# Attention steps of three, three and two key tiles in a two-layer graph network, with half-width exponentials

## The chip, the cores and the metric

The kernel runs on one core of one Trainium2 chip. The metric is the device time of one execution in microseconds (us). TensorE (PE in the profile) does the matrix products, VectorE (DVE) and ScalarE (ACT) the elementwise work, GpSimd (POOL) some elementwise work and the requests for stores, SyncE (SP) the requests for loads.

## The reference, cut to what matters

```
h = relu(layernorm(x))                                # x: 16 graphs, 1024 nodes, 256 channels
A = 1 - 2*|sigmoid(c_j - c_i) - 0.5|                  # c: mean over channels of h
q = relu(para * (h^T @ (adj * A)))                    # 4 heads of 64 channels
k, v = h @ kv_w
x = x + softmax(q k^T * scale) v                      # attention, per graph and head
h = relu(layernorm(x))
agg = A_hat @ h;  y = relu(batchnorm(agg @ W1^T));  x = x + batchnorm(y @ W2^T)
```

All of it is in float32. The attention is 16 graphs x 4 heads x 1024 queries x 1024 keys.

## The kernel before, in words

The program has a start (layer norm, keys, values and queries of the first graph), an attention stage over all 16 graphs, and an ending in `second` (the second batch norm and the last product). This study is about the attention stage.

**Units.** A unit is one graph `b`, one pair of heads `k` and one half `f` of the queries (512 of them): 16 x 2 x 2 = 64 units. In a unit, scores are made with keys on the partitions: for each of 8 tiles of 128 keys, `scores` (matmul at L1081) multiplies the tile's keys with 512 queries, for both heads `e` and both halves `c` of the tile. The four matmuls use four 64x64 quarters of the PE array. The result `sc` is 128 partitions x 1024 numbers (head 0, head 1), two banks of PSUM. One ScalarE instruction (L1089) takes the exponential of all 1024 into an SBUF tile `p`. `Unit.values` (L1124) multiplies `p` with the values `v` and accumulates over the 8 tiles into `o`. `Unit.add` (L1110, L1113) sums the `p` tiles on VectorE for the softmax's denominator; `fold` (L1159, L1160) reduces that sum, and `sums` is a small PE product (L1173) of what is left, followed by three small VectorE operations (L1181 to L1187).

**Steps.** `attention` goes through the units in steps. A step is two key tiles, so that a unit has 4 steps and the stage has 256. The order that a step gives to PE is written out by hand: first the scores of the step's two tiles; then what stands in `at_mid` (the small `sums` product); then the values of the step before; then background products, taken from the generator `background(b)` until its cost `done` reaches what is `due` at this step; then what stands in `at_end` (the folds). ScalarE and VectorE get their instructions in the same order, and each engine works its own list strictly in order.

**Background.** While the attention of graph `b` runs, `background(b)` makes the keys (`pk`), queries (`pg`) and values (`pv`) of graph `b + 1`, and the aggregation (`pa`) and hidden layer (`py`) of graph `b - 1`. All of these go through the helper `product` (L174), which uses two 128x64 halves of the array. `weigh` makes the eight weight tiles `w` of a graph: two Abs (L508) and one Tanh (L516) on ScalarE and one product with `adj` (L495) on VectorE for each.

**Buffers.** [...] `ps_sc` holds two score tiles of two banks each, `ps_o` one, `ps_mm` three for all other products. The pool `p4` holds four buffers for `p`. A score tile's buffer is written again once the exponential that reads it has ended; a `p` buffer once the values product and the VectorE sum have read it.

```
for m in (2 * g, 2 * g + 1):                       # a step's two tiles
    sc = ps_sc.tile([P, 2, FB], ...)               # two banks
    ... four matmuls into sc ...
    pr = p4.tile([P, 2, FB], ...)
    nc.scalar.activation(pr, sc, AF.Exp)           # 1024 numbers a partition
```

A trailing part `layers(True)` is a second form of both layers that is run only if a check on the softmax sums fails; in the profiled execution it is not run.

## Time and profile before

| what | value |
|---|---|
| median of 3 runs | 2460.21 us (2460.09 to 2460.84) |
| the profiled execution, its own time | 2460.34 us |
| its span, first to last instruction | 2458.6 us |
| PE busy | 2412.4 us, 98% of the span |
| VectorE busy | 2003.9 us, 82% |
| ScalarE busy | 1257.7 us, 51% |
| GpSimd busy | 559.5 us, 23% |
| exponentials (L1089) | 512 of 1020 ns |
| score matmuls (L1081), value matmuls (L1124) | 498.6 us and 494.7 us busy |
| mean granted TensorE clock | 0.993 |

A float32 matmul of the program appears in the trace as two records, each with its own weight load, so 2048 score matmuls show as 4096. Records that run side by side in different parts of the array overlap, and "busy" is the time in which at least one runs. PE's records have a modelled end: where the end of one overlaps the start of the next, the pace is read from the starts.

The span has four stretches: the start up to 54.1 us, the first graph's attention up to about 160 us, fifteen more graphs, and from about 2150 us the ending. Graphs 2 to 13 repeat every 134.4 us almost to the nanosecond.

### The profile page before, as it was taken

What the parts mean: (1) busy time and instruction counts of PE and PEld (TensorE: products, weight loads), DVE (VectorE), ACT (ScalarE), POOL (GpSimd) and SP (SyncE); (2) the same over time, 40 slices, a digit from 0 to 9 for tenths busy, and PEclk for the clock granted to TensorE, in tenths of its full rate; (3) what the DMA queues carried; (4) which work ended last, traced back from release to release, by engine and by line L of the source; (5) the groups of instructions that cost most, each with busy time, mean ns of one, the idle gap of its engine ahead of it and who ended that gap; (6) DMA issues with size and microseconds to landing.
All of it is one profiled execution on the core that took longest, in us unless ns stands there. A gap on an engine that the chain in (4) does not pass through costs nothing. (4 is left out here: it accounts for less than half of the span.)

```text
span 2458.6 us, 35932 instructions
## 1 busy us (share of the span) xinstructions
PE 2412.4 (98%) x13290; PEld 832.6 (34%) x13290; DVE 2003.9 (82%) x3103; ACT 1257.7 (51%) x1870; POOL 559.5 (23%) x645
## 2 busy tenths in 40 slices
PE   9999999999999999999999999999999999999994
PEld 4333333333333333333333333333333332334444
DVE  5678888988888888888898888888888878767775
ACT  7874554545464545445454546454454534335554
POOL 1381202111111212020211212121202103136652
PEclk9999999999999999999999999999999999999997
DMA  4675545363645554453536355544545353456559
GB/s 146 204 242 182 172 138 179 118 229 125 209 139 193 171 189 163 158 171 126 209 117 231 120 201 160 197 164 167 172 134 188 116 201 142 152 197 230 196 193 372
DMA packets 204553, 437.18 MB, mean 178 GB/s; under 512 B 21456, under 2 KB 96720, under 8 KB 200272
## 3 DMA queue, kind: packets, MB, share of 16 engines
q1 hardware_dynamic: 173328, 327.29, 39.7%
q0 software_dynamic: 31040, 107.50, 11.6%
q8 instruction: 107, 1.75, 0.3%
q14 instruction: 78, 0.64, 0.1%
HBM read 331.36 MB, written 103.35 MB: 177 GB/s over the span
## 5 line engine op out<-in xcount | busy, mean ns | idle before, releaser
L1089 ACT ACTIVATE p<-sc 128x1024 f32<-128x1024 f32 x512 | 495.4, 1020 | 649.5 <-PE sc L1081 649.5
L1113 DVE TENSOR_TENSOR acc<-acc,p 128x1024 f32<-128x1024 f32 x384 | 469.8, 1223 | 58.2 <-ACT p L1089 36.9
L1081 PE MATMUL sc<-q,k 64*64 64x512 f32 x4096 | 498.6, 602 | 0.5 <-ACT p L1089 0.5
L1124 PE MATMUL o<-p,v 128*64 128x512 f32 x2048 | 494.7, 604 | 0.0
L174 PE MATMUL pa<-aht,h_b 128*64 128x512 f32 x1536 | 346.0, 592 | 1.1 <-ACT h_b L368 1.1
L174 PE MATMUL pg<-w,x_h 128*64 128x512 f32 x1472 | 332.0, 592 | 0.0
L1081 PEld LDWEIGHTS sc<-q,k 64*64 64x64 f32 x4096 | 131.5, 132 | 336.4 <-issue 287.8
L1124 PEld LDWEIGHTS o<-p,v 128*64 128x64 f32 x2048 | 124.6, 136 | 297.7 <-issue 251.2
L1142 POOL DMA_DIRECT2D out_d<-os x58 | 32.9, 568 | 803.2 <-DVE os L1138 803.2
L495 DVE SCALAR_TENSOR_TENSOR w<-w,adj 128x1024 f32<-128x1024 f32 x128 | 164.9, 1288 | 46.1 <-ACT w L516 45.1
L174 PEld LDWEIGHTS pa<-aht,h_b 128*64 128x64 f32 x1536 | 110.1, 137 | 220.6 <-issue 207.8
L174 PEld LDWEIGHTS pg<-w,x_h 128*64 128x64 f32 x1472 | 105.7, 137 | 210.1 <-issue 198.4
L508 ACT ACTIVATE w<-cbc,csum 128x512 f32<-128x512 f32 x256 | 170.3, 716 | 0.0
L516 ACT ACTIVATE w<-w 128x1024 f32<-128x1024 f32 x128 | 135.6, 1059 | 2.5
L571 DVE TENSOR_TENSOR w<-w,w 128x1024 f32<-128x1024 f32 x112 | 134.6, 1232 | 1.5
L174 PE MATMUL pv<-kvw_f,ht 128*64 128x256 f32 x1024 | 116.1, 379 | 0.0
L174 PE MATMUL pk<-ht,kvw_f 128*64 128x512 f32 x512 | 115.2, 593 | 0.2 <-ACT ht L430 0.2
L174 PE MATMUL py<-at,w 128*64 128x512 f32 x464 | 112.6, 593 | 0.8 <-DVE at L729 0.7
L174 PE MATMUL py<-at,w1s 128*64 128x512 f32 x448 | 107.9, 595 | 0.0
L1453 ACT ACTIVATE yin_f<-yin_f,sm_f 128x512 f32<-128x512 f32 x128 | 93.5, 803 | 19.0 <-DMA yin_f<-y_d 17.0
L826 POOL DMA_DIRECT2D y_d<-y x112 | 61.6, 550 | 145.1 <-DVE y L846 75.8
L1160 DVE TENSOR_REDUCE part<-acc 128x16 f32<-128x512 f32 x128 | 87.8, 686 | 4.4
(197 smaller groups left out, 2968.6 us busy)
## 6 DMA issues: line engine op xcount, KB each, us to landing
aht<-aht_d SPq DMA_DIRECT2D x224, 512.0 KB
adj<-in_adj_dram SPq DMA_DIRECT2D x128, 512.0 KB
y_d<-y POOLq DMA_DIRECT2D x128, 256.0 KB, 3.0
yin_f<-y_d SPq DMA_DIRECT2D x32, 1024.0 KB
para<-in_para_dram SPq DMA_DIRECT2D x64, 256.0 KB
x_d<-x_x POOLq DMA_DIRECT2D x16, 1024.0 KB, 5.1
xo_f<-x_d SPq DMA_DIRECT2D x32, 512.0 KB
out_dram<-xo_f POOLq DMA_DIRECT2D x32, 512.0 KB, 11.1
```

Of the source, the lines that this page charges most:

```text
L174: nc.tensor.matmul(dst[r], left[:, r], right, start=start, stop=stop)
L495: nc.vector.scalar_tensor_tensor(w, w, 1.0, a, op0=ALU.add, op1=ALU.mult)
L508: nc.scalar.activation(w[:, t, :].rearrange("p (t q) -> p t q", q=P), cbc[:, q * NT // NH : (q + 1) * NT // NH], AF.Abs, bias=csum[:, th * ...
L516: nc.scalar.activation(made[i], made[i], AF.Tanh, scale=-0.5 / C)
L571: nc.vector.tensor_sub(block(i)[part], block(x)[part], block(y)[part])
L826: nc.gpsimd.dma_start(out=y1_d[i][:, j, :], in_=y)
L1081: nc.tensor.matmul(sc[part, e, :], ks[b][k][r, m * P + c * HW : m * P + (c + 1) * HW], qs[b][k][r, f * FB : (f + 1) * FB], start=True, sto ...
L1089: nc.scalar.activation(pr, sc, AF.Exp)
L1113: nc.vector.tensor_add(self.acc, self.acc, pr)
L1124: nc.tensor.matmul(self.o[r, :], vs[b][k][:, m, r], pr[:, e, :], start=(m == 0), stop=(m == NT - 1),)
L1160: nc.vector.tensor_reduce(self.part[:, e, :], acc.rearrange("p (c s) -> p c s", s=SQ), AX.X, ALU.add)
L1453: nc.scalar.activation(y, y, AF.Relu, bias=sh[:, j : j + 1], scale=scale[:, j : j + 1])
```

## The change

A unit has three steps, of three, three and two key tiles, in place of four steps of two: the stage has 192 steps. `scores` now takes a PSUM buffer of one bank for each head of a tile, from a pool of four such buffers (the same four banks as before), and makes the exponential of each head by its own instruction of 512 numbers. The `p` tiles come from a pool of five buffers. The `sums` product moves from the middle of a step (after the scores) to the end of the step before it, behind the background products. In `background`, the generator `w` of the weight tiles is advanced by two slots ahead of the keys' products, and by two more with the queries' first product. `due` counts key tiles in place of steps. To make room, the transposed copies `sq` are made and stored in halves, the small tiles of `degrees` live in a part of `stats1` that is not yet in use, and the channel sums are padded in the tile that they are transposed in, by GpSimd. The second form of the layers (`shifted_attention`) takes the same buffers.

```diff
         p4 = attn.enter_context(tc.tile_pool(name=f"p4_{kind}", bufs=4, side="right"))
+        p6 = attn.enter_context(tc.tile_pool(name=f"p6_{kind}", bufs=5, side="right"))
         ps_sc = attn.enter_context(
-            tc.tile_pool(name=f"ps_sc_{kind}", bufs=2, space=PSUM, side="right")
+            tc.tile_pool(name=f"ps_sc_{kind}", bufs=4, space=PSUM, side="right")
         )
...
-            for k in range(CC):
-                sq = p1.tile([P, N], F32, tag="sq", name=f"sq_{b}_{k}")
+            for q in range(2 * CC):
+                k, i = divmod(q, 2)
+                sq = p1.tile([P, FB], F32, tag="sq", name=f"sq_{b}_{q}")
...
-                nc.gpsimd.dma_start(out=hsq_d[b][:, k], in_=sq)
-                for _ in range(3):
+                nc.gpsimd.dma_start(out=hsq_d[b][:, k, i * FB : (i + 1) * FB], in_=sq)
+                for _ in range(2):
                     yield 0.0
...
-            nc.vector.transpose(turned, wides[b])
+            nc.gpsimd.memset(turned[:, NT:], 0.0)
+            nc.gpsimd.tensor_copy(turned[:, :NT], csums[b])
+            nc.vector.transpose(turned, turned)
...
+        GROUPS = (0, 1, 2), (3, 4, 5), (6, 7)
...
             yield from weave(islice(products, 6), (0, islice(w, 2)))
-            yield from weave(islice(products, 3), (0, islice(w, 1)))
+            yield from weave(islice(products, 3), (0, islice(w, 2)))
             gathered(b, 1)
-            yield from weave(islice(products, 3), (0, islice(w, AHEAD - 3)))
+            yield from weave(islice(products, 2), (0, islice(w, AHEAD - 4)))
...
                 w, products, norm = weighers[b + 1], keys_values(b + 1), normed(b - 1)
+                yield from islice(w, 2)
                 yield from weave(islice(products, 4), (0, islice(w, 4)))
                 asked = queries(b + 1)
-                yield from weave(islice(asked, 7), (0, double(w)))
+                yield from weave(islice(asked, 7), (1, double(w)))
...
-            for m in (2 * g, 2 * g + 1):
-                sc = ps_sc.tile([P, 2, FB], F32, tag="sc", name=f"sc_{b}_{k}_{f}_{m}")
+            for m in GROUPS[g]:
+                pr = p6.tile([P, 2, FB], F32, tag="p", name=f"p_{b}_{k}_{f}_{m}")
                 for e in range(2):
+                    sc = ps_sc.tile([P, FB], F32, tag="sc", name=f"sc_{b}_{k}_{f}_{m}_{e}")
                     r = slice(e * HD, (e + 1) * HD)
                     for c in range(2):
                         part = slice(c * HW, (c + 1) * HW)
                         nc.tensor.matmul(
-                            sc[part, e, :],
+                            sc[part, :],
...
-                pr = p4.tile([P, 2, FB], F32, tag="p", name=f"p_{b}_{k}_{f}_{m}")
-                nc.scalar.activation(pr, sc, AF.Exp)
+                    nc.scalar.activation(pr[:, e, :], sc, AF.Exp)
                 made.append(pr)
...
-                    due = total * (s % per_graph + 1) / per_graph
+                    whole = CC * NH * NT
+                    past = (NH * unit.at[1] + unit.at[2]) * NT + GROUPS[g][-1] + 1
+                    due = total * past / whole
...
-                            wait = 6 if opens else 4
-                            at_mid.setdefault(s + 3 + opens, []).append(last.sums)
+                            wait = 5 if opens else 3
+                            at_end.setdefault(s + 2 + opens, []).append(last.sums)
```

More of the change, by code (lines that the diff above doesn't have):

```diff
@@ L124, in layers @@
         invs = {}
-        csums, wides, cbcs, weighted, weighers, steps = {}, {}, {}, {}, {}, {}
+        csums, cbcs, weighted, weighers, steps = {}, {}, {}, {}, {}
         s1s = {}
@@ L202, in layers @@
         nc.sync.dma_start(out=kvw, in_=kv_w.rearrange("(k p) j -> p k j", p=P))
-        rows = big.tile([P, NH, NT], F32, name="rows")
+        spare = stats1[:, HC - 1].rearrange("p a s -> p (a s)")[:, (B * NH - 10) * 6 :]
+        rows = spare[:, : NH * NT].rearrange("p (q t) -> p q t", t=NT)
         def columns_of(col, name):
@@ L227, in load_adj_t @@
             return tile_
-        deg_sm = big.tile([P, 6, NT], F32, name="deg")
+        dinv = big.tile([P, NT], F32, name="dinv")
         later = {}
-        row, diag, col, deg, tmp_deg, dinv = (deg_sm[:, i, :] for i in range(6))
+        row, diag, col, deg, tmp_deg = (
+            spare[:, (NH + i) * NT : (NH + i + 1) * NT] for i in range(5)
+        )
         def degrees():
@@ L331, in __init__ @@
                 if first:
-                    wide = p2.tile([P, SQ], F32, tag="csum", name=f"csum_{b}")
-                    nc.gpsimd.memset(wide[:, NT:], 0.0)
-                    wides[b] = wide
-                    self.csum = csums[b] = wide[:, :NT]
+                    self.csum = csums[b] = p2.tile([P, NT], F32, tag="csum", name=f"csum_{b}")
                 if early:
@@ L432, in squares @@
         def squares(b):
-            for k in range(CC):
-                sq = p1.tile([P, N], F32, tag="sq", name=f"sq_{b}_{k}")
+            for q in range(2 * CC):
+                k, i = divmod(q, 2)
+                sq = p1.tile([P, FB], F32, tag="sq", name=f"sq_{b}_{q}")
+                cols = slice(q * HW, (q + 1) * HW)
                 nc.vector.transpose(
-                    sq.rearrange("p (i t s) -> p i t s", i=NS, s=SQ),
-                    hs["a", b][:, :, k * P : (k + 1) * P].rearrange("p t (i s) -> p i t s", s=SQ),
-                )
-                nc.gpsimd.dma_start(out=hsq_d[b][:, k], in_=sq)
-                for _ in range(3):
+                    sq.rearrange("p (i t s) -> p i t s", t=NT, s=SQ),
+                    hs["a", b][:, :, cols].rearrange("p t (i s) -> p i t s", s=SQ),
+                )
+                nc.gpsimd.dma_start(out=hsq_d[b][:, k, i * FB : (i + 1) * FB], in_=sq)
+                for _ in range(2):
                     yield 0.0
@@ L1031, in shifted_attention @@
                     name = f"{b}_{hd}_{t}"
-                    sc = ps_sc.tile([P, N], F32, tag="sc", name=f"sc_{name}")
+                    scs = [
+                        ps_sc.tile([P, FB], F32, tag="sc", name=f"sc_{name}_{g}") for g in range(NH)
+                    ]
                     for g in range(NH):
                         nc.tensor.matmul(
-                            sc[:, g * FB : (g + 1) * FB],
+                            scs[g],
                             qs[b][k][r, t * P : (t + 1) * P],
@@ L1040, in shifted_attention @@
                         )
-                    sm = p2.tile([P, 3], F32, tag="smx", name=f"smx_{name}")
-                    nc.vector.tensor_reduce(sm[:, 0:1], sc, AX.X, ALU.max, negate=True)
-                    pr = p4.tile([P, N], F32, tag="p", name=f"p_{name}")
-                    nc.scalar.activation(
-                        pr, sc, AF.Exp, bias=sm[:, 0:1], accum_out=sm[:, 1:2]
-                    )
-                    nc.vector.reciprocal(sm[:, 2:3], sm[:, 1:2])
-                    pt = p4.tile([P, N], F32, tag="p", name=f"pt_{name}")
+                    sm = p2.tile([P, 6], F32, tag="smx", name=f"smx_{name}")
+                    for g in range(NH):
+                        nc.vector.tensor_reduce(sm[:, g : g + 1], scs[g], AX.X, ALU.max, negate=True)
+                    nc.vector.tensor_tensor(sm[:, 2:3], sm[:, 0:1], sm[:, 1:2], op=ALU.min)
+                    pr = p6.tile([P, N], F32, tag="p", name=f"p_{name}")
+                    for g in range(NH):
+                        nc.scalar.activation(
+                            pr[:, g * FB : (g + 1) * FB],
+                            scs[g],
+                            AF.Exp,
+                            bias=sm[:, 2:3],
+                            accum_out=sm[:, 3 + g : 4 + g],
+                        )
+                    nc.vector.tensor_add(sm[:, 5:6], sm[:, 3:4], sm[:, 4:5])
+                    nc.vector.reciprocal(sm[:, 2:3], sm[:, 5:6])
+                    pt = p6.tile([P, N], F32, tag="p", name=f"pt_{name}")
                     for g in range(NH):
@@ L1119, in values @@
                     self.o = ps_o.tile([P, FB], F32, tag="o", name=f"o_{self.name}")
-                for i, pr in enumerate(prs):
-                    m = 2 * g + i
+                for m, pr in zip(GROUPS[g], prs):
                     for e in range(2):
@@ L1130, in values @@
                         )
-                if g == NG - 1:
+                if g == len(GROUPS) - 1:
                     self.os = p2.tile([P, FB], F32, tag="os", name=f"os_{self.name}")
@@ L1242, in attention @@
             units = [Unit(b, k, f) for b in range(B) for k in range(CC) for f in range(NH)]
+            NG = len(GROUPS)
             steps = [(u, g) for u in units for g in range(NG)]
@@ L1260, in attention @@
                     made = scores(*unit.at, g)
-                    due = total * (s % per_graph + 1) / per_graph
+                    whole = CC * NH * NT
+                    past = (NH * unit.at[1] + unit.at[2]) * NT + GROUPS[g][-1] + 1
+                    due = total * past / whole
                     if b == B - 1:
-                        due -= 0.5 * min(s % per_graph + 1, (per_graph - 1 - s % per_graph) * 0.75)
+                        due -= 0.25 * min(past, (whole - past) * 0.75)
                 else:
```

## The prediction

> **What bounds the kernel now.** I read the page's engine line first, then the busy time of three stretches of one graph each.

> ```profile
> PE 2412.4 (98%) x13290; PEld 832.6 (34%) x13290; DVE 2003.9 (82%) x3103; ACT 1257.7 (51%) x1870; POOL 559.5 (23%) x645
> ```
> ```profile
> 698.40:832.80 134.40, 134.40 (x782) 43.38 (x780) 115.67 (x179) 68.21 (x104) 22.62 (x31) 1.00 0.49 168
> 832.80:967.10 134.30, 134.30 (x778) 43.37 (x776) 115.65 (x179) 68.10 (x104) 22.52 (x31) 1.00 0.50 169
> ```

> In the second fence the columns are the stretch, its length, then busy us of PE, PEld, DVE, ACT, POOL. PE is busy for all of 134.4 us: in the steady graphs nothing but PE's own work sets the time. ScalarE (68 us) and VectorE (116 us) have room. The waits of PE show how little it waits for ScalarE in the whole run:

> ```profile
> PE sc L1081 <- ACT p L1089: 0.5, 1, 0.5
> ```

> But busy PE is not PE at its pace. The timeline of one step, us from the span's start, length, engine:

> ```profile
> 1001.12 1.95 PE L1081 MATMUL sc<-q,k 64*64 64x512 f32 x16
> ...
> 1002.28 1.94 ACT L1089 ACTIVATE p<-sc 128x1024 f32<-128x1024 f32 x2 [3.44 <-PE sc L1081]
> 1003.00 1.94 PE L1124 MATMUL o<-p,v 128*64 128x512 f32 x8
> ...
> 1004.77 5.32 PE L174 MATMUL pg<-w,x_h 128*64 128x512 f32 x24
> ...
> 1010.02 1.95 PE L1081 MATMUL sc<-q,k 64*64 64x512 f32 x16
> ```

> The weight loads of `pg` in that timeline start at 1004.34, 1004.77, 1005.20: one pass of 512 columns each 0.429 us. The starts then price a step. Scores, 4 passes: 1003.00 - 1001.12 = 1.88, so 0.16 over 4 x 0.429. Values, 4 passes: 1.77, 0.05 over. Background, 12 passes: 5.25, 0.10 over. **A step costs 0.31 us beyond its passes**, at the changes between the 64x64 and the 128x64 shape of the array.

> The last thing to see is the one wait of PE for an exponential. In the first unit two steps follow each other with no work between, so a third score tile stands behind two full buffers:

> ```profile
> 54.09 1.95 PE L1081 MATMUL sc<-q,k 64*64 64x512 f32 x16
> ...
> 55.47 1.92 ACT L1089 ACTIVATE p<-sc 128x1024 f32<-128x1024 f32 x2
> 56.52 0.21 PEld L1081 LDWEIGHTS sc<-q,k 64*64 64x64 f32 x8 [1.37 <-ACT p L1089]
> 56.52 2.00 PE L1081 MATMUL sc<-q,k 64*64 64x512 f32 x16 [0.49 <-ACT p L1089]
> ```

> The third tile was due at 54.09 + 4 x 0.429 + 0.05 = 55.85 and began at 56.52, 0.05 us after the first exponential's own record ended (56.47). That is what every three-tile step of the changed kernel will meet, in halves.

> [...] the four quarters start 7 ns apart, but no run here shows two halves of a tile started half a microsecond apart. [...]

> **Part 1: fewer steps (a gain).** 64 units x 1 step less x 0.31 us = 20 us off PE, all on the path. The passes are the same. Bounds 18 to 20.5.

> **Part 2: the third tile (a loss).** Six one-bank scores are asked for in one go, four banks exist, PE works in order. Time from a step's first score:
> - Tile 0's exponential starts at 1.16 (1002.28 - 1001.12) for both heads, so about 1.15 for head 0 alone.
> - A 512-wide exponential is not in the trace. From copies out of PSUM, 128x256 takes 376 ns and 128x512 584, so 512 elements are 0.416 us and the exponential 1.02 - 0.42 = 0.60. Two neighbours take 1.92, not 2.04, so the next starts 0.12 before the end, 0.48 after the start. [...]
> - Head 0 is read from 1.15 to 1.75, head 1 from 1.63 to 2.23. With 0.05 to answer, PE may write the two banks at 1.80 and 2.28.
> - They are due at 1.77. Head 0 is on time; **head 1 is 0.50 late**. Its weight load, no longer hidden, adds the 0.05 seen in the 2.00 us of the waiting pair above against 1.95. I take 0.54; bounds 0.45 (part of the load hidden)[...].

> Two of a unit's three steps have three tiles: 128 steps x 0.54 = 69 us. Behind the waiting score on PE stand the values of the step before and all background; nothing may pass. A two-tile step fits its four banks and waits for nothing.

> **Part 3: ScalarE late at a step's start.** What stands ahead of a three-tile step's exponentials now adds to PE's time one for one. The trace of before has such places: in graphs 2 to 13 the first exponential starts 1.83 us after its score in a graph's second step and 3.72 in the third, all others within 1.64. Asking for the weights ahead of the keys takes that away. In the changed order the second step has ahead of it three weight tiles (2.3 us each by the starts of L508 and L516) and four copies (0.48), 8.9 us, done by 13.7 after the step before began (the last copy waits for its product at 12.2); PE needs 3.3 for scores, 1.8 for values and 8.6 for background = 13.7 and the exponential can start 1.15 later. So 0 there, and if it fails at most 2.5 x 16 = 40. In the first graph the third step stands behind 5.5 weight tiles, four `k` copies and two of `ht`, about 3.3 us late: with its neighbours 5 us once, bounds 0 to 12.

> **Part 4: `sums` at a step's end.** It costs the same two changes of work less one of shape: scores and values with it between take 3.76 us now (at 1035.03) against 3.65. I take 0, bounds -2 to +2. But it is asked for about one and a half steps after the last fold instead of two. VectorE starts its sums at most 5.8 us behind the exponentials' ends (over all tiles of the trace), the fold takes 1.4 (two of 0.69), and the two-tile step between takes some 8; only in the first and the last two graphs, with steps of 5 to 7 us, can PE wait for it: 2 us, bounds 0 to 10.

> **Part 5: work beside PE.** ScalarE: 1024 x 0.48 against 512 x 0.90, 31 us more of 1200 idle. In the second of the three-tile steps the third `p` waits for the values of the step before (five buffers, six tiles): ScalarE stands about 1 us with copies of background products behind it, which have three `ps_mm` banks of 1.7 us each as cover. Transposes in halves: 52 x 0.70 for 26 x 1.24, 4 us of VectorE; 26 stores more on GpSimd's queue, 15 us of 1900 idle. GpSimd's padding puts up to 1 us ahead of one VectorE transpose in each graph, where VectorE idles 19 us. The weight tiles' `adj` loads are asked for earlier on SP, ahead of the `para` and x loads, and needed ten us later: 0, cover the keys' products. The tiles of `degrees`: 0.

> **Sum**, against the profiled execution: 2460.3 - 20 + 69 + 5 + 2 = **2516 us**. It stands 0.1 above the median shown, so the same holds for the median. The bounds together (wait 58 to 78, saved 20.5 to 18, the rest -2 to +24) reach from 2495 to 2544.

> **Rivals.**
> - *The banks come free in time* (faster). If exponentials release a bank before 1.77 us, part 1 alone is left: 2460 - 20 = 2441. It decides at 0.16 us of wait a step (20 / 128): below that the kernel is faster. For it: head 0 is already on time. Against: no exponential of the 256 steps started before 1.15, and 0.48 + 0.60 cannot follow in 0.62. 0.08.
> - *The late half does not run beside the early one.* If head 1's passes must wait until head 0's have left the array, 0.43 more a step, 55 us: 2571. For it: such a start is not in the trace. Against: quarters run side by side and records of both heads overlap. 0.08.
> - *Late copies and sums.* Stalls of part 3 and 4 at their upper end in many graphs, some 24 us: 2540. VectorE at 86% in the steady graphs speaks for it, its idle 19 us against. 0.12.
> - *No change to tell*: 0.02 (a difference under 0.2% is about what a measurement of this kernel cannot tell from none).

> **How the numbers follow.** My forecast has 0.70. The range takes its bounds and most of the late case, 2495 to 2546, and leaves out both outer rivals. Slower by over 0.2%: 0.70 + 0.08 + 0.12 = 0.90; within 0.02; faster 0.08.

> **What would show it.** In the changed profile: the wait of `sc` for the exponential `p` on PE, from one to some 128 in number, adding to 60 to 75 us of later starts (the view shows less, since a record's modelled end covers 0.2); values starting about 3.27 us after a three-tile step's first score; exponentials of 0.60 us; a steady graph of 134.4 - 1.25 + 4.3 = 137.5 us; 192 steps with 0.31 between passes. A steady graph under 134 would refute part 2, one near 141 would mean the second rival, waits for VectorE on PE the third.

## The result: slower, and by far more than predicted

The changed kernel takes **2654.15 us** (median of 4 runs, 2651.01 to 2655.58) against 2460.21 us for the kernel before: a ratio of 1.0786, 95% interval 1.0767 to 1.0805. The profiled execution took 2651.01 us, its span is 2649.1 us. The prediction was 2516 us with a range of 2495 to 2546. The sign was right; 138 us of loss were not foreseen.

The engine line of the page after, and the busy time of graphs 5 and 6 (the stretch, its length, busy us of PE, PEld, DVE, ACT, POOL, then the granted clock, the DMA share and GB/s):

```profile
PE 2496.1 (94%) x13290; PEld 875.1 (33%) x13290; DVE 2030.5 (77%) x3129; ACT 1296.2 (49%) x2382; POOL 569.6 (22%) x685
```
```profile
782.13:927.72 145.59, 140.02 (x779) 46.12 (x778) 117.83 (x182) 70.74 (x136) 24.54 (x34) 0.98 0.45 156
927.72:1072.62 144.90, 139.19 (x779) 45.89 (x776) 118.13 (x182) 70.97 (x136) 24.61 (x34) 0.99 0.47 157
```

Three things differ from the two lines shown of before. A steady graph takes 145 us in place of 134.4; the forecast was 137.5. PE is no longer busy all the time: 5.6 us of each graph are gaps. And the clock is below 1.00. VectorE has only 2.2 to 2.5 us more work in a graph and idles for 27 us of it, so a rise in its work alone does not explain 10 us. From the starts of the first scores of each graph, the loss of the profiled execution, 191 us, lies here: 39.7 us in graph 0, 12.5 in graph 1, 128 in graphs 2 to 13 (10.7 each), 5.1 in graph 14, the rest behind it.

The waits of PE, in the list of waits (waiter, releaser: us in total, times, longest):

```profile
PE py L175 <- DVE y L875: 71.2, 13, 5.9
PE sums L1189 <- DVE part L1176: 20.3, 1, 20.3
PE sc L1099 <- ACT p L1106: 11.8, 7, 5.4
```

The first two were not there before. Each waits for VectorE, and the list of VectorE's own waits says what VectorE stood for:

```profile
DVE sq L441 <- DMA hsq_d<-sq: 79.8, 13, 6.5
DVE csumt L472 <- POOL csumt L471: 27.3, 1, 27.3
```

**The steady graph.** The timeline of all engines in graph 6 (start, length, engine, line, operation; in brackets the idle time before and its releaser):

```profile
1043.89 0.70 DVE L441 STREAM_TRANSPOSE sq<-x_h 128x512 f32<-128x512 f32 x1
...
1044.48 1.46 SPq L193 DMA_DIRECT2D adj<-in_adj_dram  x3
1044.88 0.56 POOL L445 DMA_DIRECT2D hsq_d<-sq  x1 [1.47 <-DVE sq L441]
...
1050.63 0.71 DVE L441 STREAM_TRANSPOSE sq<-x_h 128x512 f32<-128x512 f32 x1 [6.04 <-DMA hsq_d<-sq]
...
1051.58 1.03 PE L175 MATMUL py<-at,w1s 128*64 128x512 f32 x4
...
1052.57 4.66 DVE L1130 TENSOR_TENSOR acc<-acc,p 128x1024 f32<-128x1024 f32 x3
1057.15 0.68 DVE L875 TENSOR_TENSOR y<-py,y 128x512 f32<-128x512 f32 x1
...
1057.98 1.97 PE L175 MATMUL py<-at,w1s 128*64 128x512 f32 x4 [5.37 <-DVE y L875]
```

Read it downwards. The third half of `sq` is transposed at 1043.89 and its store asked for at 1044.88. The fourth half stands right behind it in VectorE's list and needs the same, only buffer; it starts at 1050.63, when the store has landed. Behind it VectorE still owes a fold (1.4 us) and three sums of `p` (4.66 us) before it can empty the `py` bank that PE wants: PE stands 5.37 us. The store took 5.6 us to land. The first of three loads of `adj` (512 KB each) went out 0.4 us ahead of it, the others within 0.6 us behind it; in all 13 such graphs the third store, with these loads beside it, lands in 5.3 to 6.2 us, and the first, second and fourth land in 2.3 to 4.1. No run takes the loads away, so that they are what slows the store is likely, not shown. Three stretches of the same place have the clock, the DMA share and the GB/s in the last three columns, and show what comes after PE's gap:

```profile
1048.00:1051.00 3.00, 3.00 (x16) 1.01 (x14) 0.37 (x1) 1.51 (x4) 0.00 (x0) 1.00 0.99 382
...
1054.00:1057.00 3.00, 0.00 (x0) 0.00 (x0) 2.79 (x3) 0.00 (x0) 0.00 (x0) 1.00 0.00 0
...
1057.00:1060.00 3.00, 2.02 (x6) 0.85 (x8) 2.23 (x5) 0.00 (x0) 1.27 (x1) 0.61 0.03 5
```

The DMA engines are at 0.99 while the store is under way. After the gap the granted clock is down: the four records of `py` at 1057.98 take 1.97 us where the same four took 1.03 us at 1051.58. The granted clock is 0.50 for 3.4 or 6.8 us, by turns, once in each of graphs 1 to 13.

**Graph 0.** The timeline there:

```profile
160.65 0.58 POOL L299 DMA_DIRECT2D aht_d<-one  x1
161.22 0.14 POOL L470 MEMSET csumt<- 128x24 f32 x1
161.29 0.20 POOL L471 COPY csumt<-csum 128x8 f32<-128x8 f32 x1
...
161.52 0.21 DVE L472 STREAM_TRANSPOSE csumt<-csumt 128x32 f32<-128x32 f32 x1 [27.25 <-POOL csumt L471]
...
165.00 0.43 PE L1189 MATMUL sums<-part,same 128*64 128x32 f32 x4 [20.32 <-DVE part L1176]
```

Through the whole of VectorE's wait GpSimd is building `aht`, without a pause over 0.61 us, up to 161.22 (and goes on with it behind the padding); the padding of `csum` stands behind that in its list, VectorE's transpose stands behind the padding (in these 27.25 us VectorE runs nothing else), the fold behind the transpose, `sums` behind the fold, and all of PE behind `sums`.

**The step itself** is as forecast. A three-tile step in the timeline of PE and of its weight loads:

```profile
1009.21 3.34 PE L1099 MATMUL sc<-q,k 64*64 64x512 f32 x24
1012.48 2.79 PE L1140 MATMUL o<-p,v 128*64 128x512 f32 x12
```
```profile
1010.98 0.20 PEld L1099 LDWEIGHTS sc<-q,k 64*64 64x64 f32 x4 [0.71 <-ACT p L1106]
1011.47 0.20 PEld L1099 LDWEIGHTS sc<-q,k 64*64 64x64 f32 x4 [0.29 <-ACT p L1106]
```

Scores to values are 3.27 us, the number forecast, and the third tile's two heads load their weights at 1010.98 and 1011.47, each 0.05 us after an exponential's end (1010.93 and 1011.42).

### The profile page after: what moved, and what is told of

Read it like the earlier page. It is cut to its first block, busy times and chain, and to the rows that moved or that the text cites. A ratio compares the mean times of both kernels' runs of the same rounds, so it can differ in the third digit from the quotient of the medians.

```text
span 2649.1 us, 36668 instructions
## 1 busy us (share of the span) xinstructions
PE 2496.1 (94%) x13290; PEld 875.1 (33%) x13290; DVE 2030.5 (77%) x3129; ACT 1296.2 (49%) x2382; POOL 569.6 (22%) x685
## 3 DMA queue, kind: packets, MB, share of 16 engines
q8 instruction: 107, 1.75, 0.3%
## 5 line engine op out<-in xcount | busy, mean ns | idle before, releaser
L1106 ACT ACTIVATE p<-sc 128x512 f32<-128x512 f32 x1024 | 528.7, 605 | 582.2 <-PE sc L1099 502.8
L1099 PE MATMUL sc<-q,k 64*64 64x512 f32 x4096 | 557.4, 608 | 11.8 <-ACT p L1106 11.8
L1130 DVE TENSOR_TENSOR acc<-acc,p 128x1024 f32<-128x1024 f32 x384 | 482.1, 1256 | 76.3 <-ACT p L1106 51.4
L1140 PE MATMUL o<-p,v 128*64 128x512 f32 x2048 | 484.3, 604 | 0.0
L1099 PEld LDWEIGHTS sc<-q,k 64*64 64x64 f32 x4096 | 149.2, 132 | 345.5 <-issue 178.1
L175 PE MATMUL py<-at,w1s 128*64 128x512 f32 x448 | 121.4, 652 | 71.5 <-DVE y L875 71.2
L1127 DVE TENSOR_TENSOR acc<-p,p 128x1024 f32<-128x1024 f32 x64 | 78.6, 1229 | 82.4 <-ACT p L1106 82.3
L846 ACT ACTIVATE y<-py,vec 128x512 f32<-128x512 f32 x28 | 19.3, 688 | 226.2 <-PE py L175 226.2
L175 PE MATMUL py<-at,w 128*64 128x512 f32 x464 | 128.7, 666 | 0.8 <-DVE at L735 0.7
L369 ACT ACTIVATE h_b<-x_x,lnsm_b 128x256 f32<-128x256 f32 x128 | 70.0, 602 | 87.7 <-DVE lnsm_b L358 87.7
```

The source lines that it names most:

```text
L175: nc.tensor.matmul(dst[r], left[:, r], right, start=start, stop=stop)
L369: nc.scalar.activation(self.h[:, t, :], self.src[:, t, :], AF.Relu, bias=self.sm[:, 1, t : t + 1], scale=self.sm[:, 0, t : t + 1], accum_o ...
L1099: nc.tensor.matmul(sc[part, :], ks[b][k][r, m * P + c * HW : m * P + (c + 1) * HW], qs[b][k][r, f * FB : (f + 1) * FB], start=True, stop=True,
L1106: nc.scalar.activation(pr[:, e, :], sc, AF.Exp)
L1127: nc.vector.tensor_add(self.acc, self.held, pr)
L1130: nc.vector.tensor_add(self.acc, self.acc, pr)
```

## The experiments

The theory after this reading: three separate losses. (a) The fourth half of `sq` behind the third through one buffer: in steady graphs, with the halved clock that follows. (b) The padding on GpSimd: graph 0. (c) The third tile's bank wait, as predicted. Its rival for (a): VectorE is late because three-tile steps bunch its sums of `p`. For (b): the loads of `degrees` or the changed order of weights hold graph 0.

| kernel | median us | ratio to before, 95% | graph 0 | graph 3 |
|---|---|---|---|---|
| changed | 2654.15 | 1.0767 to 1.0805 | 145.2 | 145.8 |
| sq_in_y | 2557.27 | 1.0378 to 1.0413 | 145.5 | 137.7 |
| pad_dve | 2628.63 | 1.0665 to 1.0700 | 126.8 | 145.6 |
| both | 2532.55 | 1.0276 to 1.0310 | 121.5 | 137.7 |
| two_tile | 2462.58 | 1.0001 to 1.0018 | 105.5 | 134.4 |
| before_halves2 | 2572.33 | 1.0427 to 1.0471 | 105.5 | 143.3 |
| before_pad2 | 2491.73 | 1.0110 to 1.0144 | 136.4 | 134.4 |
| twos_first2 | 2517.54 | 1.0220 to 1.0254 | 105.9 | 137.7 |
| values_between2 | 2509.95 | 1.0186 to 1.0220 | 121.4 | 136.5 |
| late_half | 2532.17 | 1.0271 to 1.0306 | 122.2 | 137.7 |
| keys_first | 2545.12 | 1.0331 to 1.0366 | 118.7 | 138.7 |
| whole_exp | 2529.89 | 1.0265 to 1.0299 | 118.6 | 137.6 |

The last two columns are us from the first score of that graph to the first of the next. The kernel before has 105.5 and 134.4 there; graphs 2 to 13 of "both" have 137.7 but for two of 138.0 and 139.1.

**1. sq_in_y: another buffer for the halves**

```diff
-                sq = p1.tile([P, FB], F32, tag="sq", ...)
+                sq = py.tile([P, FB], F32, tag="y", ...)     # ring of seven
```

> The changed kernel with one edit: the four halves of squares take their buffer from the ring of seven y buffers of the same size instead of the single sq buffer. Theory (VectorE stands behind the store that must leave the single buffer, PE then waits for py banks and its clock is halved): the wait of the squares' transpose for its store, 80 us in 13 waits, is gone; the wait of py for L875 on PE falls from 71 us to under 8; no halved clock in graphs 2 to 13; a steady graph takes 137.4 us instead of 145.0; the sum is 12 x 7.6 and 9.5 for graph 1, so about 2654 - 100 = 2554 us. Rival (VectorE is simply late because three-tile steps bunch its sums of p): py still waits for VectorE, a steady graph stays above 142, 2610 to 2654 us.

Measured 2557.27 us, a steady graph of 137.7 us; the wait of `py` for L875 is gone, and no halved clock stands in graphs 1 to 13. The theory holds for (a): 97 us. The fourth transpose now starts 0.63 us behind the third: so close do the two writes follow each other where nothing holds the second.

**2. pad_dve: the padding off GpSimd**

```diff
-            nc.gpsimd.memset(turned[:, NT:], 0.0)
-            nc.gpsimd.tensor_copy(turned[:, :NT], csums[b])
+            nc.vector.memset(turned[:, NT:], 0.0)
+            nc.vector.tensor_copy(turned[:, :NT], csums[b])
```

> The changed kernel with one edit: the padding of csum (a memset and a copy) is on VectorE instead of GpSimd. Theory (in graph 0 VectorE's transpose of csumt waits 27 us for the copy, which stands on GpSimd behind the building of aht, and all of VectorE, ScalarE and PE stop behind it): the 27.3 us wait of csumt and the 20.3 us wait of the sums' product are gone, the clock stays whole there, graph 0 takes about 109 us instead of 145; in all 2654 - 36 = 2618 us; steady graphs stay at 145. Rival (graph 0 is held by the loads of the degrees' tiles or by the earlier weight tiles): the stop only moves, graph 0 stays above 130, 2640 us or more.

Measured 2628.63 us: 25.5 less, not 36. The 27.3 us and the 20.3 us waits are gone, but graph 0 still takes 126.8 us (in the profiled execution, the slowest of the four; from sq_in_y to "both" the same edit takes 24.0 us off graph 0). The padding is one cause in graph 0 and not the only one.

**3. both: edits 1 and 2 together**

> Both edits together: squares in the y ring and the padding on VectorE. If the prediction's steps for the score banks (69 us) and for the fewer steps (20 us) are right and these two stalls are all that it missed: 2654 - 100 - 36 = 2518 us, graph 0 about 109, a steady graph 137.4. If another loss stands behind them, it is over 2535; if the late score half costs less than worked out, under 2505.

Measured 2532.55 us. The two edits add up (97 + 25.5 = 122; together 121.6), and the steady graph of 137.7 us is the forecast's 137.5 within 0.2. Some 14 us more than expected are left, nearly all in graph 0.

**4. two_tile: the kernel of both edits with steps of two tiles**

```diff
-        GROUPS = (0, 1, 2), (3, 4, 5), (6, 7)
+        GROUPS = (0, 1), (2, 3), (4, 5), (6, 7)
...
-                            wait = 5 if opens else 3
+                            wait = 6 if opens else 4
```

> The kernel of both edits with steps of two tiles again (GROUPS (0,1), (2,3), (4,5), (6,7), the wait for the finish 4 and 6 steps as before), all else as changed: half-width score banks and exponentials, sums at a step's end, weights ahead of keys. By the prediction's parts 1 and 2, against the kernel of both edits +20 for the 64 steps and -69 for the third tile: about 2468 us, a steady graph of 134.4, scores to values 1.88 us in each step, no wait of sc for p on PE. Rival (the half-width exponentials or the sums at the step's end cost PE by themselves): a steady graph above 136, 2490 us or more.

Measured 2462.58 us, graph by graph the time of the kernel before (105.5, 135.6, 134.4 and so on). So half-width banks and exponentials, `sums` at a step's end and the order of the weights cost PE nothing in the attention; the 70 us that "both" loses against it are the three-tile step. Its profiled span is 2.0 us longer than that of the kernel before, and 1.9 of them lie behind the attention's last scores.

**5. before_halves2: the halves alone, in the kernel before**

```diff
-            for k in range(CC):
-                sq = p1.tile([P, N], F32, tag="sq", ...)
+            for q in range(2 * CC):
+                k, i = divmod(q, 2)
+                sq = p1.tile([P, FB], F32, tag="sq", ...)
...
-                for _ in range(3):
+                for _ in range(2):
```

> The kernel before with one part of the change alone: squares turned in four halves through a single half-width sq buffer instead of two full ones. If the single buffer is the fault by itself, VectorE stands some 6 us in each of graphs 1 to 13 behind the store, PE waits some 5 us for a py bank and its clock is halved after it: a steady graph of about 142 us instead of 134.4, 2460 + 100 = 2560 us. Rival (it needs the three-tile step, whose three sums of p of 1.2 us each stand behind the late transpose): PE waits under 1 us a graph, a steady graph of at most 135.5, 2460 to 2476 us.

Measured 2572.33 us, steady graphs of 141.0 to 143.4. The halves lose 112 us without any three-tile step; the rival falls. Its waits of PE, and the one of VectorE behind them:

```profile
PE py L174 <- DVE y L853: 33.7, 13, 3.2
PE py L174 <- DVE y L871: 27.4, 13, 2.6
```
```profile
DVE sq L440 <- DMA hsq_d<-sq: 86.1, 13, 7.2
```

**6. before_pad2: the padding alone, in the kernel before**

The edit of the change (memset and copy on GpSimd where the transpose is, no padding ahead), nothing else.

> The kernel before with one part of the change alone: csum padded on GpSimd at the place of its transpose. If GpSimd's backlog of the building of aht is what VectorE waits for in graph 0, VectorE stands 15 to 27 us once, graph 0 takes 120 to 135 us instead of 105.5, all others stay at 134.4: 2475 to 2490 us. Rival (the backlog comes from the changed order of loads and weights): no wait over 3 us, 2460 to 2463 us.

Measured 2491.73 us, just over the range given: graph 0 takes 136.4 us and every other its old time. VectorE waits 33.0 us for the copy and PE 28.8 us for `sums`. GpSimd's queue of `aht` alone does this; the order of loads and weights is not needed.

**7. twos_first2: two-tile steps in graph 0 alone**

```diff
+        def groups(b):
+            return TWOS if b == 0 else THREES
...
-            for m in GROUPS[g]:
+            for m in groups(b)[g]:
```

> The kernel of both edits with steps of two tiles in graph 0 alone and of three, three, two in all others. The rest of 16 us in graph 0 (121.5 us against 105.5) comes, by this theory, from exponentials that stand behind copies and the degrees' tiles on ScalarE, which a three-tile step on four banks passes on to PE and a two-tile step does not: graph 0 about 106, in all 2532 - 16 = 2517 us. Rival (loads or VectorE hold graph 0): graph 0 stays above 115, or graph 1 takes the loss, over 2525 us.

Measured 2517.54 us, graph 0 in 105.9 us. The rest of the loss in graph 0 (15.0 us) belongs to the three-tile steps there. In the trace of "both" most of it is two places: PE stands 3.2 us at 83.8 and 4.4 us at 146.5 behind late exponentials, and the clock is halved after each, for 3.4 and 6.8 us. At the first, the exponentials stand on ScalarE behind weight tiles. At the second, ScalarE itself stands behind the load of a tile of `degrees`:

```profile
147.64 1.06 ACT L245 ACTIVATE at<-at 128x1024 f32<-128x1024 f32 x1 [8.05 <-DMA at<-in_adj_t_dram]
```
```profile
150.91 2.46 PE L1099 MATMUL sc<-q,k 64*64 64x512 f32 x8 [4.42 <-ACT p L1106]
```

In the kernel before, ScalarE's longest wait for such a load is 3.1 us, and PE doesn't wait behind it. So the rival of (b), the loads of `degrees`, is right for this part of graph 0; why the load comes that much later isn't shown.

**8. values_between2: the third tile's scores after the values**

```diff
                     last.values(g_last, prs)
+                if s < len(steps):
+                    for pr in scores(*unit.at, g, slice(2, 3)):
+                        unit.add(pr)
+                        made.append(pr)
```

> The kernel of both edits with the scores of a step's third tile asked for after the values of the step before, all else the same. If the third tile waits for a score bank (0.54 us), 2.6 us of values cover that wait, and two more changes between kinds of product cost 0.16 us: 128 x (0.54 - 0.16) = 49 us less, 2532 - 49 = 2484 us, a steady graph of 134.7. Rival (the wait is not the bank's but the pace of ScalarE over the whole step): the values or the next step wait instead, steady graph above 136.5, over 2510 us.

Measured 2509.95 us, steady graph 136.5: half of the gain expected, at the edge between the two theories by its sum. The trace decides: in graphs 2 to 5 no third tile waits any more (two tiles of scores 1.878 us, the third 1.02), so the wait was the bank's. What the expectation had too low was the price of the two added changes: values to scores costs 0.10 more than values to background, the third tile's own change 0.16, the weight load after it 0.045, some 0.31 against the 0.55 saved; and waits for `py` take 0.5 us a graph more.

**9. late_half: one half-width buffer, another place**

```diff
-            yield from squares(b)
+            yield from squares(b, range(2 * CC - 1))
...
             gathered(b, 0)
-            yield from weave(islice(products, 6), (0, islice(w, 2)))
+            yield from islice(products, 2)
+            run(squares(b, (2 * CC - 1,)))
+            yield from weave(islice(products, 4), (0, islice(w, 2)))
```

> The changed kernel with the padding on VectorE, and with the single half-width sq buffer kept; the fourth half of squares is turned two of the next products later, after the first gather of ht is asked for, instead of right behind the third. If the fault was that the fourth half is asked for right behind the third, whose store has not left the only buffer, some more cover is enough: no wait over 2 us of VectorE for the store, a steady graph of 137.7 us as with the y ring, 2532 us in all. Rival (a half buffer is too small wherever the halves stand): VectorE still waits 3 us or more once a graph, a steady graph above 140, over 2560 us.

Measured 2532.17 us, a steady graph of 137.7, as with seven buffers. VectorE has no wait for the store left. Timeline of VectorE and GpSimd in a steady graph, these lines alone:

```profile
983.42 0.70 DVE L441 STREAM_TRANSPOSE sq<-x_h 128x512 f32<-128x512 f32 x1
984.41 0.56 POOL L445 DMA_DIRECT2D hsq_d<-sq  x1 [1.47 <-DVE sq L441]
...
990.47 0.69 DVE L875 TENSOR_TENSOR y<-py,y 128x512 f32<-128x512 f32 x1 [0.45 <-PE py L175]
...
991.94 0.70 DVE L441 STREAM_TRANSPOSE sq<-x_h 128x512 f32<-128x512 f32 x1
```

The slowest of these stores still takes 6.1 us to land, but 8.5 us now lie between the third and the fourth transpose, and VectorE works through its fold, its sums and two evacuations of `py` in them. One half-width buffer is enough where its writes stand far enough apart. The fault of (a) is that the fourth write follows the third by less than the landing of a store; more buffers (sq_in_y) or more distance (this run) both take it away.

**10. keys_first: weights behind the keys again**

The changes to `prepare` and to the first lines of `background` undone, in the kernel of both edits.

> The kernel of both edits with the weights asked for behind the keys again, as in the kernel before. By the prediction's part 3 the exponentials of a graph's second and third step then start about 0.7 and 2.6 us late, and in three-tile steps PE waits as long: up to 3.2 us in each of graphs 1 to 14, 2532 + 14 x 3.2 = 2577 us, a steady graph up to 140.9. Rival (background products between two steps cover it): under 138.2, 2532 to 2540 us.

Measured 2545.12 us, 12.6 more than "both", a steady graph of 138.7 but for two: between the two expectations. One step in each graph has scores to values of 4.28 us in place of 3.27. Weights ahead of keys is worth about 1 us a graph, not 3.2, since the longer step covers most of the delay that the kernel before showed.

**11. whole_exp: two-bank scores, one exponential of 1024 in three-tile steps**

```diff
-                    sc = ps_sc.tile([P, FB], F32, tag="sc", ...)          # in a pool of four
...
-                    nc.scalar.activation(pr[:, e, :], sc, AF.Exp)
+                sc = ps_sc.tile([P, 2, FB], F32, tag="sc", ...)           # in a pool of two
+                nc.scalar.activation(pr, sc, AF.Exp)
```

> The kernel of both edits with score tiles of two banks and exponentials of 1024 elements as before, in steps of three, three and two tiles. Tile 0's exponential then ends 1.16 + 1.02 = 2.18 us after its first score and frees both banks, which are due at 1.77: the third tile waits 0.46 + 0.05 = 0.51 us, where two exponentials of 512 made it wait 0.55: 128 x 0.04 = 5 us less and 31 us less of ScalarE, 2520 to 2530 us, scores to values 3.23 us. Rival (each half that comes free lets PE begin, so that halves are worth 0.4 us a step): scores to values 3.6 us, 2570 us or more.

Measured 2529.89 us, scores to values 3.25 us. The timeline of PE and ScalarE in one such step:

```profile
1004.74 1.95 PE L1098 MATMUL sc<-q,k 64*64 64x512 f32 x16
...
1005.89 1.94 ACT L1105 ACTIVATE p<-sc 128x1024 f32<-128x1024 f32 x2 [2.34 <-PE sc L1098]
...
1006.97 1.09 PE L1098 MATMUL sc<-q,k 64*64 64x512 f32 x8 [0.28 <-ACT p L1105]
```

The third tile starts 2.23 us after the first, 0.06 after the first exponential's end by its 1.02 us. So dividing banks and exponentials in two, the part of the change that was to let banks come free sooner, gains nothing in a three-tile step: the second head's bank comes free no earlier (its weights load at 2.26 us in the step shown of the changed kernel) than both do together.

No version among these beats the kernel before. With the wait, a three-tile step loses more than the missing step saves; without it (values_between2), the added changes between kinds of product and the longer waits for `py` still cost more than the missing step saves, 136.5 us a graph against 134.4.

## Why the prediction was wrong

**What bounds the kernel (right).** PE's own order sets the steady graph: with the stalls gone ("both"), the largest wait of PE for VectorE is that of `py`, 4.2 us over 13 graphs.

**Part 1, fewer steps, 20 us (right as far as the runs tell).** It can't be seen alone. With 0.55 us a wait (next point) the steady graph of 137.7 leaves 8 x 0.55 - 3.3 = 1.1 us for four steps less, against the 1.24 used.

**Part 2, the third tile, 69 us (right).** In graphs 2 to 5 of "both", scores to values of a three-tile step average 3.290 us. Without a wait it would be 1.878 + 2 x 0.429 = 2.736, so the wait is 0.554 us; 0.54 was used. The exponential of 512 takes 605 ns; the estimate was 0.60. The 78 us at the upper end of the bounds for this wait were an estimate of the author's that no trace of before shows. The rival of banks free in time (2441) and that of halves that don't run side by side (2571, 3.7 us) are both refuted by the 3.27 us.

**Part 3, ScalarE late (too small in the first graph).** Steady graphs: 0, as said. The term "with its neighbours 5 us once, bounds 0 to 12" measures about 12. twos_first2 gets back 15.0 us; of these 8 x 0.55 = 4.4 are the third tile's waits of part 2, and four more steps take back 1.2 of part 1: 15.0 - 4.4 + 1.2 = 11.8. The sum counted one place with its neighbours, and neither the clock that is halved behind the stand (3.4 and 6.8 us in "both") nor the second place, where ScalarE waits 8.1 us for a load; part 5 had put the tiles of `degrees` at 0.

**Part 4, `sums` at a step's end (right in the attention, and its 2 us were not needed).** two_tile has it, and its graphs take the old time; in "both" PE has no wait for VectorE at `sums`. The wait of 20.3 us that the changed kernel shows on `sums` is not the fold being late by its own work, as this part bounded it, but the padding.

**Part 5, work beside PE costed at nothing (the step that failed).** Two of its sentences carry 122 of the 138 us missed. Of the other 16, some 7 lie in graph 0 (part 3), 4 in graphs 2 to 13 (137.7 against 137.5, and two slower graphs) and 3 behind the attention, where the prediction had nothing.

- "Transposes in halves: 52 x 0.70 for 26 x 1.24, 4 us of VectorE; 26 stores more on GpSimd's queue" priced the instructions and their queues, and not the wait that the change adds: four writes through one buffer in place of two. The trace of before had one side of it: 26 stores of the full width that land in 3.0 to 8.4 us, with 8.8 us from the first transpose to the second (1068.7 and 1077.5). The other side is in the changed order: the third write stands 3.6 us behind the second and the fourth, where nothing holds it, 0.63 us behind the third, and no store of the changed trace lands in under 2.3 us. It cost 97 us: 5.5 us of PE waiting in each of 13 graphs, and after it a clock of 0.50 for 3.4 or 6.8 us.
- "GpSimd's padding puts up to 1 us ahead of one VectorE transpose in each graph, where VectorE idles 19 us" took the price of the padding for the wait for it. In steady graphs this holds. In graph 0 GpSimd has a long queue, the building of `aht` (from 105 to 167 us), and the padding stands behind most of it: 25 us.

With both mended and graph 0 kept at two tiles (twos_first2), the kernel takes 2517.5 us; the forecast of parts 1 to 4 was 2516. That these are so close is in part luck: with graph 0 at two tiles the prediction's own terms give 2516 - 4.3 + 1.2 - 5 = 2508.

**Late copies and sums (rival three).** It named waits for VectorE on PE as its sign, and these appeared. Its argument, VectorE's load, was not the cause: VectorE was 81% busy in the slow steady graph, and of the time that it stood still 6 us were behind the store; the halves alone, with two-tile steps (before_halves2), bring the same waits. Its 24 us were far from 122.

## What to carry to other kernels

Where an edit shrinks a buffer or moves a small operation to another engine, price the wait and not the instruction: for a buffer, the time between two writes in the writer's list against the slowest landing of the transfer that must leave it (0.63 us in sq_in_y, against up to 6.2 in the changed kernel); for an engine, the longest queue that it has anywhere in the run (here the building of `aht`, for which VectorE stood 27.25 us). A wait passed on to what stood behind it in the engine's list, however idle the engine was on average: VectorE, idle for 27 us of a steady graph, waited 6.04 us for a store, and PE stood 5.37 us behind it. And when a stall can't be avoided, moving the instruction a few places down the list can hide it without a byte more of memory (late_half: 8.5 us between the two writes, 137.7 us a graph in place of 145).

## What the runs showed of the hardware that was not expected

Worked out over the attention in all 13 traces (some 8000 slices of the grid, with the modelled ends of PE's records), the clock went from full to half behind every slice in which PE stood for more than 1.91 of the 3.41 us, and behind three below that (1.4 to 1.8). In the changed kernel alone, PE stood for 2.35 us or more in the slices with such a halving behind them, and for 1.91 at most in the other slices at full clock. Seen on this grid, the same gap of 5.2 to 5.9 us that costs 3.4 us of halved clock in one graph and 6.8 in the next fills one slice but for 0.1 us at most; in the slice behind that PE still stood 1.2 to 2.0 us where the clock stayed halved, and at most 0.6 where it did not.

PE works for 4.2 us on the mean in such a stretch, so half speed (1.97 us for the four records of `py` that took 1.03) costs about 2.1 us of a graph's 7.3; over a quarter of this stall's price was not the stall.
